# Search for the 256th score: thresholds and base formed on ScalarE instead of VectorE

## The chip, the cores and the metric

The kernel runs on one core of a Trainium2 chip. The core has five engines, each with its own queue of instructions that it works off in order: TensorE (PE, matrix products, with its weight loads shown as PEld), VectorE (DVE), ScalarE (ACT), GpSimd (POOL) and SyncE (SP, which only starts transfers here). They wait for each other by semaphores. The metric is the time of one execution on the device, in microseconds (us); the time before is the median of three runs.

## The reference

Two layers of a small transformer on 2048 tokens of width 512, in float32. Layer 0 adds a linear attention and a mixture of 16 experts to its input. Layer 1 adds a causal softmax attention over a window of 1024 and a block that works only on the highest-scoring eighth of the tokens. The change lies in that last block, where the 256 tokens are chosen (its weights' names shortened):

```python
xn = _layernorm(x, axis=-1)
x = x + attn(xn, ...) + ffn(xn, ...)
# in ffn:
k = max(1, int(T * CAPACITY))                        # 256
scores = jnp.einsum('btd,d->bt', hidden_states, w_router)
_, idx = jax.lax.top_k(scores, k)
idx = jnp.sort(idx, axis=-1)
sel = hidden_states[b, idx]
...
output = hidden_states.at[b, idx].set(gated.reshape(B, k, D))
```

What must come out of the search is the set of the 256 highest of 2048 scores, ties to the earlier token.

## The kernel before

The kernel goes through stages: layer 0 (to about 720 us in the profiled execution), then a stage here called the projections (720 to about 1010 us), the work on the chosen tokens, and last the attention of layer 1.

The projections run over 16 tiles t of 128 tokens. For each tile PE forms three products of 128 x 512, q, k and v (`p`, line 965, four quarters each, two passes per quarter), into a ring of three PSUM buffers. `normed_qk` normalises q and k: ACT squares (`t`, 754), DVE sums (`rr`, 755), ACT takes the root (78), DVE inverts (79) and multiplies (`qk`, 758), POOL applies the rotary embedding (763 to 773). One tile later `turned_qk` transposes them on PE (`trqk`, 110), and ACT copies the result out of PSUM (117) into qT and kT. The next tile's input is transposed in the same way (`tr`, copy to `xnt`).

Beside this two other pieces of work are threaded through the same tiles, step by step, at places written out in the loop:

- `early`, the row maxima of the attention to come (`maxima`): PE forms scores `pa` (633, masks 639 and 641) in one PSUM buffer, DVE reduces them to `mx` (645). Each pa waits for the mx before it. Per tile a few small reductions (`nm`, `parts`, 649 to 653) follow, then a transpose on PE (`tn`, 658).
- `route`, the choice of the tokens (`routing`). The scores are turned into whole numbers that order the same, split into a high half and a low half of 16 bits. `largest` finds the 256th largest of 2048 such numbers in three rounds, first for the high half (names ending in _h), then for the low half (_l). Each number of a round is tried by one partition: partition p forms the threshold base + step x (p + 1) (`thr`, 850; `steps` holds step x (p + 1)), compares all 2048 values with it and counts them (`ge`, `cnt`, 853), and notes whether there are at least 256 (854). A product with a matrix of ones on PE (`pc`, 859) sums the 128 notes into every partition; base rises by that sum times the step (860). The steps are 512, 4 and 1. The 2048 values come to every partition by way of DRAM: `row_d` is written from the scores' layout and read back as `row`, once for each half, by SP's transfers.

After the high half POOL forms the candidates of the low half from base (`low`, `above`, 867 to 870), and after the low half the set and the places (873 and on).

Four kinds of result share one PSUM buffer, `ps_t` with the tag "tr" and one buffer: tr, trqk, tn and pc. PE can write the next of them only when the one before has been read.

The code is written in one order, but the instructions of each engine are put in order by a scheduler when the kernel is built, so that a change of engine can also move instructions around it. At run time each queue is fixed.

Of the kernel before, what the change touches and what calls it, by code (L numbers as in the profile page):

```python
# [14 lines left out]
AF = mybir.ActivationFunctionType  # L15
ALU = mybir.AluOpType
# [22 lines left out]
def two_layer_kernel(ctx: ExitStack, tc: tile.TileContext, a: dict, out: bass.AP):  # L39
    nc = tc.nc  # L40
    V, S, G, PE = nc.vector, nc.scalar, nc.gpsimd, nc.tensor
# [4 lines left out]
    def const(shape, name, pool=cpool, dtype=F32):  # L46
        return pool.tile(shape, dtype, tag=name, name=name)
# [21 lines left out]
    def load(eng, dst, src):  # L69
        eng.dma_start(out=dst, in_=src)  # L70
# [57 lines left out]
    with ExitStack() as l0:  # L128
# [15 lines left out]
        with ExitStack() as p1:  # L144
# [8 lines left out]
            def load_x(t):  # L153
# [24 lines left out]
                base=0, channel_multiplier=0,  # L178
# [158 lines left out]
        with ExitStack() as p3:  # L337
# [119 lines left out]
            steps = head.steps()  # L457
# [7 lines left out]
            for b in range(NTB):  # L465
                atT, sh, xl = head.atT, head.sh, head.xl
                if b < NTB - 1:
                    head = Head(b + 1)
                    steps = chain(steps, head.steps())
# [253 lines left out]
    with p4:  # L723
# [59 lines left out]
        def routing():  # L783
# [5 lines left out]
                base=0, channel_multiplier=-1,  # L789
# [19 lines left out]
            def small(name, n=NT, dtype=F32):  # L809
                return const([P, n], name, r5, dtype)  # L810

            STEPS = (512, 4, 1)
            steps = const([P, 3], "steps", r5)
# [25 lines left out]
            def largest(m, first, name):  # L839

                load(nc.sync, row_d, m)
                row = r5.tile([P, NT * P], F32, tag="row", name=f"row_{name}")
                load(nc.sync, row, row_d.rearrange("p t -> (p t)").partition_broadcast(P))
                base = small(f"base_{name}", 1)
                G.memset(base, float(first))
                for _ in range(4):
                    yield
                for k, step in enumerate(STEPS):
                    thr = wk.tile([P, 1], F32, tag="thr", name=f"thr_{name}{k}")
                    V.tensor_tensor(thr, steps[:, k : k + 1], base, ALU.add)  # L850
                    ge = r5.tile([P, NT * P], BF16, tag="ge", name=f"ge_{name}{k}")
                    cnt = wk.tile([P, 1], F32, tag="cnt", name=f"cnt_{name}{k}")
                    V.tensor_scalar(ge, row, thr, None, ALU.is_ge, ALU.add, accum_out=cnt)
                    V.tensor_scalar(cnt, cnt, K2 - 0.5, None, ALU.is_ge)
                    yield
                    yield

                    pc = ps_t.tile([P, 1], F32, tag="tr", name=f"pc_{name}{k}")
                    PE.matmul(pc, ones, cnt, start=True, stop=True)
                    V.scalar_tensor_tensor(base, pc, float(step), base, ALU.mult, ALU.add)  # L860
                    yield
                return base

            th = yield from largest(hi, -32768, "h")

            low, above = small("low"), small("above")
            G.tensor_scalar(low, hi, th, None, ALU.is_equal)
            G.tensor_tensor(low, low, lo, ALU.mult)
            G.tensor_scalar(above, hi, th, 1e6, ALU.is_gt, ALU.mult)
            G.tensor_tensor(low, above, low, ALU.add)  # L870
            tl = yield from largest(low, 1, "l")
            same, inc, turn = small("same"), small("inc"), small("turn")
            G.tensor_scalar(above, low, tl, None, ALU.is_gt)
# [634 lines left out]
```

## Time and profile before

| | |
|---|---|
| three runs | 1710.59, 1710.7, 1712.12 us |
| median | 1710.7 us |
| the profiled execution | 1707.93 us |
| its span, first to last instruction | 1706.2 us |
| mean granted clock of PE in it | 0.994 |
| 740 to 850 us: busy PE / DVE / ACT / POOL | 101.0 / 71.0 / 23.8 / 51.9 us of 110 |
| 850 to 960 us: the same | 105.5 / 72.0 / 23.9 / 64.7 us of 110 |

The durations of the search's own instructions in that execution:

| line | engine | what | count | us each |
|---|---|---|---|---|
| 850 | DVE | thr | 6 | 0.15 in three of high half; 0.15, 0.36 and 2.34 in low |
| 853 | DVE | compare and count, 2048 values | 6 | 2.33 to 2.35 |
| 854 | DVE | cnt | 6 | 0.15 |
| 859 | PE | pc, two passes | 6 | 0.28 to 0.34 |
| 860 | DVE | base | 6 | 0.15 |

The profile lists, for each group of instructions, what ended the idle time before it ("<-"). The time of an engine that is idle while it is not needed costs nothing; what counts here is the idle time of PE, and the share of its clock that was granted.

### The profile page before, as it was taken

The numbers are of one execution on the slowest core, as the hardware profiler recorded it, in microseconds if no ns is written. First come the engines' busy times: TensorE is split into PE (matmuls) and PEld (weight loads), VectorE is DVE, ScalarE is ACT, GpSimd is POOL, SyncE is SP. The second block draws the span as 40 slices with busy tenths as digits, with TensorE's granted clock in tenths as the row PEclk, the third lists the DMA queues.
The fourth block names the chain that finished last, engine by engine and source line by source line (L and its number), as shares of the span: only waits on it lengthen the run. The fifth ranks groups of instructions, "written<-read, shape, count | busy, mean of one in ns | idle before, by whom it ended". The sixth has DMA issues, their size and how long they took to land.

```text
span 1706.2 us, 20420 instructions
## 1 busy us (share of the span) xinstructions
PE 1658.3 (97%) x8114; PEld 744.2 (44%) x8114; DVE 972.9 (57%) x1240; ACT 596.2 (35%) x955; POOL 499.6 (29%) x398
## 2 busy tenths in 40 slices
PE   8999999999999999999999989999999999999999
PEld 3445444444444444444443434454564333433343
DVE  4755646344445544356566676775554477556565
ACT  3213333243253344222121220440100576447473
POOL 3230000000000200053565425230000677558584
PEclk9999999999999999999999999999899999999999
DMA  9411001120030431121011034112222300110101
GB/s 362 168 38 47 25 25 37 46 90 25 25 111 25 94 105 50 51 68 56 25 27 31 28 105 167 62 50 75 74 99 75 100 1 2 50 51 2 50 2 38
DMA packets 62384, 109.22 MB, mean 64 GB/s; under 512 B 12529, under 2 KB 14065, under 8 KB 61521
## 3 DMA queue, kind: packets, MB, share of 16 engines
q1 hardware_dynamic: 55856, 106.12, 18.4%
q0 software_dynamic: 1152, 1.21, 0.4%
q10 hardware_dynamic: 5280, 0.59, 0.4%
q8 instruction: 63, 1.03, 0.2%
q14 instruction: 33, 0.26, 0.1%
HBM read 86.24 MB, written 21.67 MB: 63 GB/s over the span
## 4 chain that ended last, share of the span: by engine, by line
PE 83%; DVE 10%; ACT 2%; issue 2%; POOL 1%; DMA 1%; SPq 0%; DVEq 0%; POOLq 0%; ACTq 0%
PE eg L492 6%; PE ea L494 6%; PE acc L478 6%; PE pa L633 6%; PE ps L1300 6%; PE p L965 6%; PE av L1374 6%; PE po L553 3%; PE pq L367 3%; PE po L1344 3%; PE gx L242 3%; DVE mx L645 3%; PE pk L288 2%; PE mg L1214 2%; PE pm L1229 2%; PE sg L403 2%
## 5 line engine op out<-in xcount | busy, mean ns | idle before, releaser
L645 DVE TENSOR_REDUCE mx<-pa 128x4 f32<-128x1536 f32 (+3 forms) x144 | 252.8, 1756 | 160.5 <-PE pa L641 77.6
L1407 POOL TENSOR_TENSOR acc<-acc,pt 128x1024 f32<-128x1024 f32 (+2 forms) x110 | 252.7, 2325 | 96.7 <-DVE acc L1407 43.4
L1334 ACT ACTIVATE pt<-ps 128x1024 f32<-128x1024 f32 (+3 forms) x208 | 181.4, 924 | 108.1 <-PE ps L1323 61.5
L1407 DVE TENSOR_TENSOR acc<-acc,pt 128x1024 f32<-128x1024 f32 (+1 forms) x80 | 144.4, 1833 | 103.8 <-POOL acc L1407 103.8
L633 PE MATMUL pa<-kT,qT 32*128 32x384 f32 (+3 forms) x1152 | 139.8, 539 | 17.9 <-DVE mx L645 17.4
L350 ACT ACTIVATE r_e<-eg 128x512 f32<-128x512 f32 x128 | 75.8, 594 | 202.2 <-PE eg L492 195.7
L1300 PE MATMUL ps<-qT,kT 32*128 32x512 f32 (+3 forms) x1152 | 139.9, 525 | 0.0
L352 DVE TENSOR_TENSOR h<-ea,r_e 128x512 f32<-128x512 f32 x128 | 87.1, 684 | 85.1 <-ACT r_e L351 84.1
L743 POOL TENSOR_TENSOR cosg<-cosg,gam 128x512 f32<-128x512 f32 x2 | 2.5, 1264 | 442.6 <-DVE gam L740 442.6
L492 PE MATMUL eg<-xl,rwgT 128*128 128x512 f32 x256 | 130.8, 592 | 0.0
L494 PE MATMUL ea<-xw,rw1T 128*128 128x512 f32 x256 | 130.7, 592 | 0.0
L478 PE MATMUL acc<-h,rw2T 128*128 128x512 f32 x256 | 129.3, 592 | 0.0
L965 PE MATMUL p<-w_qk,xnt 128*128 128x512 f32 x256 | 124.2, 608 | 2.0 <-DVE qk L758 1.9
L1374 PE MATMUL av<-pt,v 128*32 128x512 f32 (+3 forms) x1024 | 100.8, 482 | 0.0
L1300 PEld LDWEIGHTS ps<-qT,kT 32*128 32x128 f32 x1152 | 54.7, 183 | 94.6 <-issue 65.7
L633 PEld LDWEIGHTS pa<-kT,qT 32*128 32x128 f32 x1152 | 46.6, 184 | 101.8 <-DVE mx L645 69.2
L488 DVE TENSOR_TENSOR xw<-xw,xl 128x512 f32<-128x512 f32 x64 | 43.8, 685 | 82.4 <-DMA xw<-w_d 82.2
L351 ACT ACTIVATE r_e<-r_e 128x512 f32<-128x512 f32 x128 | 80.3, 629 | 5.5 <-ACT r_e L350 1.8
L478 PEld LDWEIGHTS acc<-h,rw2T 128*128 128x128 f32 x256 | 48.7, 190 | 61.2 <-issue 53.7
L494 PEld LDWEIGHTS ea<-xw,rw1T 128*128 128x128 f32 x256 | 48.7, 190 | 61.2 <-issue 59.3
L492 PEld LDWEIGHTS eg<-xl,rwgT 128*128 128x128 f32 x256 | 48.7, 190 | 61.2 <-issue 60.7
L288 PE MATMUL pk<-k_wT,xnT 128*128 128x512 f32 x128 | 62.1, 629 | 3.6 <-ACT xnT L117 3.6
(336 smaller groups left out, 2419.7 us busy)
## 6 DMA issues: line engine op xcount, KB each, us to landing
xw<-w_d SPq DMA_DIRECT2D x64, 256.0 KB, 3.2
x<-in_x SPq DMA_DIRECT2D x16, 256.0 KB, 4.0
res_d<-x SPq DMA_DIRECT2D x16, 256.0 KB, 2.7
xr<-res_d SPq DMA_DIRECT2D x16, 256.0 KB, 4.1
xn_d<-xn SPq DMA_DIRECT2D x16, 256.0 KB, 2.9
res_d<-xr SPq DMA_DIRECT2D x16, 256.0 KB, 3.1
xnq<-xn_d SPq DMA_DIRECT2D x16, 256.0 KB, 2.7
v_d<-vt SPq DMA_DIRECT2D x16, 256.0 KB, 2.0
```

Source lines behind the costliest of these rows:

```text
L288: PE.matmul(pk, xt[:, c, :], k_wT[:, c, :], start=c == 0, stop=c == NC - 1)
L352: V.tensor_tensor(dst, pa, r, ALU.mult)
L478: PE.matmul(acc, rw2T[:, j, e, :], h, start=e == 0 and j == 0, stop=e == E - 1 and j == 1,)
L492: PE.matmul(pg, rwgT[:, e, hb], xl, start=True, stop=True)
L494: PE.matmul(pa, rw1T[:, e, hb], xw, start=True, stop=True)
L633: PE.matmul(pS[:, h, : w * P], qT[r, g, i * P : (i + 1) * P], kT[r, g, ks], start=True, stop=not (edge or last),)
L645: V.tensor_reduce(mx[:, g, :, c], pS[:, :, : w * P], AX.X, ALU.max)
L965: PE.matmul(pj, xnt[:, c, :], w, start=c == 0, stop=c == NC - 1)
L1300: PE.matmul(pS[h // 2][:, h % 2, t0 * P - q0 : (t1 + 1) * P - q0], kT[r, g, kb * P : (kb + 1) * P], qT[r, g, t0 * P : (t1 + 1) * P], start ...
L1334: S.activation(pT[:, :, :n], pS[hp][:, :, :n], AF.Exp)
L1374: PE.matmul(self.av[h * HD : (h + 1) * HD, t0 * P - o : (t1 + 1) * P - o], vs[kb // 4][:, kb % 4, hs], got[h // 2][:, h % 2, t0 * P - q0 : ...
L1407: eng.tensor_tensor(part, part, got[hp][:, :, : q1 - q0], ALU.add)
```

## The change

Two lines of `largest` change engine. The threshold was a DVE addition of `steps` and `base`; it becomes an ACT instruction, the identity function with base as its bias. The new base was a DVE instruction, pc x step + base; it becomes an ACT identity with step as scale and base as bias. Both act on one number per partition. The compare, the count and the product with ones stay.

```diff
@@ -847,7 +847,8 @@
                     yield
                 for k, step in enumerate(STEPS):
                     thr = wk.tile([P, 1], F32, tag="thr", name=f"thr_{name}{k}")
-                    V.tensor_tensor(thr, steps[:, k : k + 1], base, ALU.add)
+
+                    S.activation(thr, steps[:, k : k + 1], AF.Identity, bias=base)
                     ge = r5.tile([P, NT * P], BF16, tag="ge", name=f"ge_{name}{k}")
                     cnt = wk.tile([P, 1], F32, tag="cnt", name=f"cnt_{name}{k}")
                     V.tensor_scalar(ge, row, thr, None, ALU.is_ge, ALU.add, accum_out=cnt)
@@ -857,7 +858,7 @@
 
                     pc = ps_t.tile([P, 1], F32, tag="tr", name=f"pc_{name}{k}")
                     PE.matmul(pc, ones, cnt, start=True, stop=True)
-                    V.scalar_tensor_tensor(base, pc, float(step), base, ALU.mult, ALU.add)
+                    S.activation(base, pc, AF.Identity, bias=base, scale=float(step))
                     yield
                 return base
```

In the built program twelve instructions go from DVE's queue to ACT's, and the scheduler moves some others. On DVE the compare goes ahead of the small reductions (second round of the high half) and of the second qk (first round of the low half), and one mx goes ahead of rr of t=5. On PE trqk of the first and the third low round goes ahead of most of p<-w_v, one quarter of p<-w_qk behind two pa, and the products around pa of the next tiles shift by a quarter. On ACT the copy of qT goes ahead of the root of t=5. On POOL the rotary embedding of t=5 goes behind the first part of the routing after the low half. The lines after 850 have numbers greater by one in the changed kernel. Before and after these places the queues are the same.

## The prediction

> **What bounds the kernel now.** I read the page first, then TensorE's waits in the stretch of the search (740 to 850 us), then the timeline there, then the granted clock in slots of 3.4 us.
>
> ```profile
> span 1706.2 us, 20420 instructions
> PE 1658.3 (97%) x8114; PEld 744.2 (44%) x8114; DVE 972.9 (57%) x1240; ACT 596.2 (35%) x955; POOL 499.6 (29%) x398
> ```
>
> TensorE (PE) is busy for 97% of the span, so an edit is worth only what it takes from the idle time or the slow time of PE. The waits of PE, 740 to 850 us (line, who it waited for: us, times, longest):
>
> ```profile
> PE pa L633 <- DVE mx L645: 3.7, 3, 2.2
> PE trqk L110 <- DVE base_l L860: 3.3, 2, 2.1
> PE p L965 <- DVE qk L758: 1.9, 2, 1.6
> ```
>
> All of them end on VectorE (DVE), which also runs the search. The first can be due to the compare L853 ahead of the reduction mx; the second is the search itself. The timeline (start, us, engine, line, what; idle time in brackets):
>
> ```profile
> 761.28 2.35 POOL L763 TENSOR_TENSOR t<-qk,cosg 128x1024 f32<-128x1024 f32 x1 [8.16 <-DVE base_h L860]
> 761.31 2.34 DVE L850 TENSOR_TENSOR thr_l<-steps,base_l 128x1 f32<-128x1 f32 x1
> 763.57 2.33 DVE L853 TENSOR_SCALAR_CACHE_REDUCE ge_h<-row_h,thr_h 128x2048 bf16<-128x2048 f32 x1
> 766.02 1.22 DVE L645 TENSOR_REDUCE mx<-pa 128x4 f32<-128x1024 f32 x1
> 767.29 0.71 PE L633 MATMUL pa<-kT,qT 32*128 32x256 f32 x8 [0.87 <-DVE mx L645]
> ...
> 784.65 1.24 PE L633 MATMUL pa<-kT,qT 32*128 32x384 f32 x8 [2.20 <-DVE mx L645]
> ...
> 798.57 0.15 DVE L860 SCALAR_TENSOR_TENSOR base_l<-pc_l,base_l 128x1 f32<-128x1 f32 x1
> 798.87 0.63 PE L110 MATMUL trqk<-ident,qk 128*128 128x128 f32 x4 [1.26 <-DVE base_l L860]
> ...
> 817.65 0.15 DVE L860 SCALAR_TENSOR_TENSOR base_l<-pc_l,base_l 128x1 f32<-128x1 f32 x1
> 817.95 0.63 PE L110 MATMUL trqk<-ident,qk 128*128 128x128 f32 x4 [2.06 <-DVE base_l L860]
> ```
>
> First, an add of one number per partition (thr_l) took 2.34 us: it began 0.03 us after a GpSimd (POOL) tensor_tensor and ended with it; its siblings took 0.15 us. Second, the transposes trqk wait until base_l has read pc, since pc, tr, trqk and tn share one PSUM buffer (ps_t4, bufs=1), and base_l stands in DVE's queue behind a reduction of 1.75 or 2.28 us. The clock (stretch, us, busy PE, PEld, DVE, ACT, POOL, granted clock, DMA share, GB/s):
>
> ```profile
> 781.70:785.10 3.40, 1.20 (x10) 0.31 (x8) 2.86 (x4) 0.00 (x0) 3.32 (x3) 1.00 0.00 0
> 785.10:788.50 3.40, 3.40 (x17) 1.54 (x10) 1.76 (x1) 0.14 (x1) 0.51 (x1) 0.51 0.00 0
> ...
> 815.90:819.30 3.40, 1.35 (x12) 0.73 (x12) 1.90 (x2) 0.58 (x1) 3.40 (x3) 1.00 0.00 0
> 819.30:822.70 3.40, 3.40 (x14) 1.74 (x11) 2.23 (x1) 0.37 (x1) 3.32 (x2) 0.50 0.00 0
> ...
> 962.70:966.10 3.40, 1.61 (x8) 0.40 (x6) 2.91 (x5) 0.79 (x2) 0.00 (x0) 1.00 0.00 0
> ```
>
> After a slot in which PE was busy for 1.20 or 1.35 us, the next runs at half clock; after 1.61 us it did not here. So the two long gaps each cost a slow slot too. Its price by the timeline at 818.5: pa to the next p takes 1.71 us (1.31 at 807.42), two half-products 1.82 (0.86), four transposes 0.76 (0.50): 1.6 us.
>
> **The change, part by part.** Six thr (L850, DVE 0.15 us) and six base (L860, DVE 0.15 us) go from DVE to ScalarE (ACT); DVE keeps the six compares (2.34 us each) and six cnt. On ACT neither operation is in the trace. The nearest rows are the square root with a pointer as bias, 128x1, 294 ns, and the copy of 128x16 out of PSUM (ties), 172 ns; I take 0.30 for each, as the bias is a pointer here too, and 0.18 from PE's end to ACT's start (tr ends at 750.98, its copy starts at 751.16). The low end would bring each base 0.13 us sooner, the high end, rr's 321 ns, 0.02 later: under 0.4 us over three waits. ACT is busy for 23.8 of 110 us there, and the instruction order of the changed program adds no table load. A wait of ACT for pc holds up what follows it on ACT; I followed the order through, 0.03 to 0.1 us per handover, times of the trace of before:
>
> - Second round, 755 us: base and thr on ACT end at 755.2, so the compare starts as before (755.3). But nm (L649), 650 and 651 now come after it, ahead of rr: rr starts 0.3 late, qk and so PE's p at 760.59 too: **+0.3**.
> - Third round, 761 us: thr_l no longer waits for POOL. qk ends at 761.4, the compare starts at 761.5 instead of 763.57, mx at 764.4 (pa is ready then) instead of 766.02, and PE finds it done: **-0.87**.
> - base_h at 772.26 waited for mx (771.12); on ACT it ends 1.2 us sooner, so low and the two row transfers also start 1.2 sooner, and the compare for which DVE waited (row_l, 1.35 us) starts at 779.2 instead of 780.39. PE arrives 0.6 sooner as well, so its gap of 2.20 falls only to 1.6: **-0.6**. If the transfer lands no sooner it is 0; if all of 1.2 counts, -1.2.
> - First low round: trqk is now placed after one quarter of p<-w_v instead of three, and base_l on ACT behind rr (L78), which ends at 795.81: base ends at 796.1, the quarter at 795.65. Gap 1.26 becomes 0.6: **-0.66**. The compare goes ahead of the second qk here (2.4 us later); its buffer is wanted only some 5 us later, and POOL's rope of 7.2 us (763 to 773) still ends 4 us ahead of its transposes. Hidden; without that cover 2.4.
> - Second low round: a quarter of p<-w_qk moves behind pa_2, so PE comes to pa_2 0.86 sooner than before and waits for mx behind the compare: 0.65 instead of 0.1, **+0.55**.
> - Third low round: base_l directly follows the square of t=5 on ACT, trqk waits 0.2 instead of 2.06: **-1.86**. But ACT's copy of qT now precedes rr (L78), and mx of pa_2 precedes rr on DVE, so the last mx is later, and pa_0 of the next tile waits 0.3: **+0.3**. POOL's rope for t=5 moves behind the ten-odd small routing steps; it then ends at about the old time against a use 10 us later: 0.
>
> Sum of the idle time: 0.3 - 0.87 - 0.6 - 0.66 + 0.55 - 1.86 + 0.3 = -2.84. Both slow slots should go: 0.2 us of idle cannot halve the clock, and a gap of 1.6 leaves 1.8 busy in its slot, over the 1.61 that passed: -3.2. In all **-6.0 us**: 1706.2 to 1700.2 in the span of this execution (it ran 1707.93 in all). The three timed runs have their median at 1710.7, 2.8 above that execution; the difference is taken off it: **1704.7**. Bounds: a slot costs from 0 (not drawn) to 1.7 (half of 3.4), and the later gaps of about 1.8 us (964 us: full clock kept; 1000.6 us: lost) move against the slots by the gain, so one slot may come or go there: 1.6 either way.
>
> **The rivals.** (a) *The clock does not follow the gaps.* The rows for it: 1.61 us of busy time kept the full clock at 962.7 but lost it in 1000.2 to 1003.6. Then the slow slots stay and only idle time goes: 1710.7 - 2.84 = 1707.9. This is also what a rule of the Trainium skill would make of it, "TensorE: Matmul & The Clock Gate", section "Why this matters for your kernels": drops come from idle gaps above some 3 us. By that rule no gap here, 2.20 at most, should cost a slot; the trace shows two that did.
>
> (b) *The compare remains the pace.* It stays on DVE, 2.34 us, and now stands ahead of nm and qk. If the gaps at 784.65 and 798.87 stay whole, with the first slow slot, and the three new stops double from 1.15 to 2.3: -0.87 - 1.86 - 1.6 + 2.3 = -2.0: 1708.7. For it: PE's 3.7 us on mx; against it: DVE is busy for 71 of 110 us.
>
> (c) *Slower: ACT's queue holds the one PSUM buffer.* ACT works in order, and base now stands behind rr or a square that waits for others; while it waits, no tr, trqk or tn can be written. If base comes as late as rr does in the third low round (815.4 instead of 813.44: 1.9 us) in all three low rounds, with the slow slots kept: 3 x 1.9 - 0.87 - 0.6 = +4.2: 1714.9. It decides once base starts more than 2.06 us after pc, the longest such gap now. For it: the small operation is dearer on ACT (294 against 150 ns); against it: ACT is idle for 78% here and the order puts base first in two of three rounds. The Trainium skill speaks against the move too: "ScalarE: Activation LUTs", section "Rules for kernel authors", gives adds and multiplies to VectorE. By the rows that alone would be 12 x 0.144 = 1.7 us, were all on the path.
>
> (d) *It does nothing it says*: the numbers are the same whole numbers, so only if all of it were covered: 1710.7.
>
> **How the numbers follow.** The forecast 0.52, (a) 0.12, (b) 0.19, (c) 0.15, (d) 0.02. The forecast's own range is 1701 to 1707.3, from the slots and the transfer. Within 0.2% is 1707.3 to 1714.1, about what a measurement of this kernel can tell from no change. Faster: 0.52, half of (a), a little of (b): 0.60. Slower: (c), 0.15. Same: 0.25. The range of 8 in 10 reaches from 1700.5 (all row time counts, 1.2, a later slot goes too) to 1713.0, leaving out (c) and a little below.
>
> **What would show it.** Right: no thr of 2.3 us on any engine; base on ACT within 1 us of pc; the gap at 817.95 under 0.5 and full clock after it; the compare at 780 about 1 us sooner. Wrong: the waits of PE on mx between 740 and 850 us above 5 us, trqk waiting for ACT for over 1 us, or slots at half clock in the same number as before. The whole forecast falls if PE's idle time to 850 us does not shrink.

## The result and the profile after

On the chip of the first runs the changed kernel takes 1704.58 us (median of 8 runs, 1703.0 to 1710.8) against 1710.77 us (8 runs, 1708.05 to 1712.2): ratio 0.9974, 95% interval 0.9962 to 0.9986, which is 2.4 to 6.5 us less. Repeated on another chip the medians are 1703.80 and 1707.81 us, ratio 0.9973 (0.9964 to 0.9983). The profiled execution ran 1704.56 us; its page begins so (span, then busy time, share and instructions of each engine):

```profile
span 1702.2 us, 20423 instructions
PE 1655.0 (97%) x8114; PEld 742.2 (44%) x8114; DVE 969.9 (57%) x1228; ACT 598.4 (35%) x967; POOL 499.3 (29%) x398
```

The twelve instructions are on ACT. The waits of PE from 740 to 850 us (line, who it waited for: us, times, longest):

```profile
PE p L966 <- DVE qk L758: 2.3, 2, 1.8
PE pa L633 <- DVE mx L645: 2.1, 2, 1.8
PE tn L658 <- DVE parts L653: 0.4, 1, 0.4
PE trqk L110 <- ACT base_l L861: 0.2, 1, 0.2
```

They sum to 5.0 us, where the three shown of before made 8.9. The row of trqk behind base fell from 3.3 to 0.2, that of pa behind mx from 3.7 to 2.1; p behind qk did not fall. The timeline of the changed kernel at the same places (start, us, engine, line, what; idle time before in brackets):

```profile
762.75 0.27 ACT L861 ACTIVATE base_h<-pc_h,base_h 128x1 f32<-128x1 f32 x1
763.05 0.29 ACT L851 ACTIVATE thr_h<-steps,base_h 128x1 f32<-128x1 f32 x1
763.25 0.28 ACT L851 ACTIVATE thr_l<-steps,base_l 128x1 f32<-128x1 f32 x1
763.38 2.35 DVE L854 TENSOR_SCALAR_CACHE_REDUCE ge_h<-row_h,thr_h 128x2048 bf16<-128x2048 f32 x1
763.52 2.36 POOL L763 TENSOR_TENSOR t<-qk,cosg 128x1024 f32<-128x1024 f32 x1 [9.87 <-DVE qk L758]
...
781.28 2.35 DVE L854 TENSOR_SCALAR_CACHE_REDUCE ge_l<-row_l,thr_l 128x2048 bf16<-128x2048 f32 x1 [0.94 <-DMA row_l<-row_d]
785.54 0.93 PE L633 MATMUL pa<-kT,qT 32*128 32x384 f32 x8 [1.78 <-DVE mx L645]
795.36 0.63 PE L110 MATMUL trqk<-ident,qk 128*128 128x128 f32 x4 [0.21 <-ACT base_l L861]
809.16 1.14 PE L633 MATMUL pa<-kT,qT 32*128 32x512 f32 x8 [0.32 <-DVE mx L645]
812.07 0.26 ACT L861 ACTIVATE base_l<-pc_l,base_l 128x1 f32<-128x1 f32 x1
812.47 0.63 PE L110 MATMUL trqk<-ident,qk 128*128 128x128 f32 x4
```

The reader is to see four things. No thr takes 2.3 us, and the compare of the third round (763.38) stands directly behind its threshold. The gaps of 1.26 and 2.06 us ahead of the transposes are 0.21 us and nothing (the last line has no bracket). The gap of 2.20 us ahead of pa is still 1.78, because the compare there waits for its data: DVE is idle 0.94 us for row_l, 1.35 before. And ACT takes 0.26 to 0.29 us for each small operation.

The search stretch gains, and the next one gives some back (stretch, us, then busy PE, PEld, DVE, ACT, POOL, granted clock, DMA share, GB/s). The kernel before:

```profile
740.00:850.00 110.00, 101.00 (x506) 47.54 (x505) 70.95 (x92) 23.80 (x47) 51.85 (x64) 0.97 0.12 41
850.00:960.00 110.00, 105.48 (x508) 44.79 (x507) 72.03 (x68) 23.90 (x46) 64.67 (x54) 1.00 0.11 28
```

The changed kernel:

```profile
740.00:850.00 110.00, 104.95 (x542) 49.12 (x540) 71.48 (x89) 27.66 (x61) 54.58 (x66) 0.98 0.13 43
850.00:960.00 110.00, 103.81 (x496) 44.15 (x494) 71.04 (x63) 23.80 (x46) 62.81 (x52) 1.00 0.13 31
```

PE is busy 3.95 us more than before in the first stretch and 1.67 us less in the second. The waits of PE from 850 to 1020 us name the new one, which before did not have:

```profile
PE pa L633 <- DVE mx L645: 9.3, 9, 1.8
PE trqk L110 <- POOL qk L773: 2.6, 2, 2.2
```

It lies in the rotary embedding of tile 8, here in the changed kernel:

```profile
882.87 2.34 POOL L773 TENSOR_TENSOR qk<-t,t 128x1024 f32<-128x1024 f32 x1
885.26 0.66 PE L110 MATMUL trqk<-ident,qk 128*128 128x128 f32 x4 [2.17 <-POOL qk L773]
```

and here in the kernel before:

```profile
886.37 2.35 POOL L773 TENSOR_TENSOR qk<-t,t 128x1024 f32<-128x1024 f32 x1
888.77 0.66 PE L110 MATMUL trqk<-ident,qk 128*128 128x128 f32 x4
```

Before, POOL ended at 888.72 and PE began at 888.77 without a wait: just in time. After, PE was ready at 883.09, 5.7 us sooner; POOL ended at 885.21, only 3.5 sooner.

The clock in slots of 3.4 us, two stretches of the changed kernel:

```profile
743.40:746.80 3.40, 1.58 (x9) 0.58 (x7) 2.46 (x4) 1.28 (x3) 0.39 (x1) 1.00 0.21 77
746.80:750.20 3.40, 3.40 (x19) 1.67 (x22) 0.69 (x1) 0.00 (x0) 3.40 (x3) 0.50 0.02 5
...
883.30:886.70 3.40, 1.44 (x6) 0.69 (x6) 2.13 (x2) 1.17 (x3) 1.91 (x1) 1.00 0.00 0
886.70:890.10 3.40, 3.40 (x19) 1.65 (x19) 3.27 (x4) 0.06 (x1) 1.49 (x1) 1.00 0.00 0
```

The slots at half clock behind the two old gaps (785 and 819 us) are gone, and so is one behind a gap at 1002 us. A gap at 745 us, before the search's second round, costs one now, and the new gap at 885 us did not in this execution.

Half or more of what these two executions lose to the clock is lost elsewhere. Near 1200 us, long after the search, both kernels run for three slots on end at half clock (before, then after):

```profile
1190.00:1215.00 25.00, 22.15 (x97) 11.61 (x96) 12.08 (x14) 6.72 (x12) 0.00 (x0) 0.80 0.13 43
1190.00:1215.00 25.00, 22.15 (x102) 12.96 (x100) 12.37 (x15) 7.04 (x13) 0.00 (x0) 0.80 0.12 42
```

That is about 5 us each. In all thirteen profiles of this document the clock of this stretch is 0.73 to 0.86, a loss of 3.5 to 6.8 us. No experiment here touches it.

### The profile page after: what moved, and what is told of

It reads as the page before. It is cut to its first block, busy times and chain, and to the rows that moved or that the text cites. A ratio compares the mean times of both kernels' runs of the same rounds, so it can differ in the third digit from the quotient of the medians.

```text
span 1702.2 us, 20423 instructions
## 1 busy us (share of the span) xinstructions
PE 1655.0 (97%) x8114; PEld 742.2 (44%) x8114; DVE 969.9 (57%) x1228; ACT 598.4 (35%) x967; POOL 499.3 (29%) x398
## 4 chain that ended last, share of the span: by engine, by line
PE 80%; DVE 9%; POOL 3%; DMA 2%; ACT 2%; issue 2%; SPq 0%; DVEq 0%; POOLq 0%; ACTq 0%
PE eg L492 6%; PE ea L494 6%; PE acc L478 6%; PE ps L1301 6%; PE pa L633 6%; PE av L1375 6%; PE p L966 5%; PE po L553 3%; PE pq L367 3%; PE po L1345 3%; PE gx L242 3%; DVE mx L645 3%; PE mg L1215 2%; PE pm L1230 2%; PE po L555 2%
```

## The experiments

Two numbers are given for each kernel, since the slots at half clock are drawn anew in each execution and spread the times of one kernel over 3 to 10 us. The median and the ratio are the time itself. The *full-clock time* is the span of each run times its mean granted clock, averaged over the runs: what the span would be with no slow slot. It is an estimate, good to some 0.2 to 0.7 us by the scatter of its mean. "Lost" is the mean of span minus full-clock time. The kernels of one chip are held against the runs of the kernel before on that chip.

| kernel | runs | median us | ratio (95%) | lost us | full-clock us | against before |
|---|---|---|---|---|---|---|
| chip A: before | 27 | 1706.52 | | 7.3 | 1697.7 | |
| e1_thr_act | 11 | 1708.64 | 1.0014 (1.0005 to 1.0023) | 9.9 | 1696.9 | -0.8 |
| e2_base_act | 11 | 1704.77 | 1.0000 (0.9990 to 1.0010) | 8.8 | 1694.5 | -3.2 |
| e3_thr_one | 11 | 1704.77 | 0.9992 (0.9982 to 1.0003) | 7.4 | 1696.2 | -1.5 |
| e4_after_z5 | 5 | 1699.38 | 0.9964 (0.9950 to 0.9978) | 6.8 | 1692.0 | -5.7 |
| chip B: before | 27 | 1707.81 | | 8.0 | 1698.0 | |
| e5_after_again | 10 | 1703.80 | 0.9973 (0.9964 to 0.9983) | 7.7 | 1694.9 | -3.2 |
| e6_after_held | 12 | 1702.99 | 0.9974 (0.9963 to 0.9985) | 7.8 | 1693.5 | -4.6 |
| e7_hyb_z5_held | 5 | 1699.60 | 0.9948 (0.9935 to 0.9961) | 6.8 | 1690.9 | -7.1 |
| e8_before_z5 | 12 | 1709.49 | 1.0002 (0.9993 to 1.0011) | 8.8 | 1698.2 | +0.2 |
| chip C: before | 23 | 1707.28 | | 7.9 | 1697.3 | |
| e9_after_thrice | 12 | 1704.11 | 0.9987 (0.9975 to 0.9999) | 7.7 | 1694.7 | -2.6 |
| e10_hyb_z5 | 8 | 1701.80 | 0.9971 (0.9956 to 0.9985) | 7.2 | 1692.7 | -4.6 |
| e11_after_z5_again | 8 | 1700.79 | 0.9963 (0.9951 to 0.9975) | 6.4 | 1692.3 | -5.0 |

The profiled executions give a second measure of the queues. It is the time from the p that waits for qk at 745.21 us to two later pa, those at 875.00 and 910.98 us in the kernel before, less 1.7 us (half of 3.4) for each slot at half clock in between. The wait for POOL near 885 us lies between the two pa. It is an estimate from one execution each; two profiles of one kernel differ in it by up to 0.4 us.

| kernel | to the pa ahead of POOL's wait | to the pa behind it |
|---|---|---|
| before | 126.4 | 162.4 |
| e1_thr_act | 125.9 | 161.9 |
| e3_thr_one | 125.7 | 161.7 |
| e2_base_act | 122.8 | 159.0 |
| after | 121.7 | 159.8 |
| e5_after_again | 121.8 | 159.8 |
| e4_after_z5 | 121.6 | 157.6 |
| e11_after_z5_again | 121.2 | 157.2 |
| e10_hyb_z5 | 121.6 | 157.6 |
| e9_after_thrice | 123.2 | 159.2 |

### One half of the change alone: the threshold

```diff
-                    V.tensor_tensor(thr, steps[:, k : k + 1], base, ALU.add)
+                    S.activation(thr, steps[:, k : k + 1], AF.Identity, bias=base)
```

> Only the threshold on ScalarE, base stays on VectorE. The order on PE is that of the kernel before. Theory (two separate parts; the threshold was held by GpSimd's use of the shared path): thr_l is 0.3 us and no longer 2.34, the compare of the third high round starts 2 us sooner, PE's wait of 0.87 us on mx near 767 goes, the two waits of trqk on base_l (1.26 and 2.06 us) and the clock slots behind the long gaps stay. Time 0.9 us under before, 1709.8. Rival (it is the whole change that counts, or load on VectorE in general): half of the gain, 3 us, 1707.7.

The blocked threshold goes, and with it the wait at 767 us, but the three gaps stay (timeline of this kernel):

```profile
783.97 0.93 PE L633 MATMUL pa<-kT,qT 32*128 32x384 f32 x8 [2.54 <-DVE mx L645]
798.25 0.63 PE L110 MATMUL trqk<-ident,qk 128*128 128x128 f32 x4 [1.26 <-DVE base_l L860]
817.33 0.63 PE L110 MATMUL trqk<-ident,qk 128*128 128x128 f32 x4 [1.70 <-DVE base_l L860]
```

0.8 us of full-clock time is gained, the size of the wait removed (0.87), and 0.5 us in the traces. Part of it is spent at once: the gap ahead of pa at 784 grows from 2.20 to 2.54 us. The median rose, with 9.9 us lost to the clock, and the ratio's interval lies above 1; this half alone is no gain in time.

### The other half alone: the base

```diff
-                    V.scalar_tensor_tensor(base, pc, float(step), base, ALU.mult, ALU.add)
+                    S.activation(base, pc, AF.Identity, bias=base, scale=float(step))
```

> Only base on ScalarE, thresholds stay on VectorE. The order on PE is that of the changed kernel. Theory: trqk's waits on base_l fall to 0.2 us each, row_l comes about 1 us sooner, the slot at half clock behind the old gap of 2.06 goes, but thr_l or thr_h in the third high round still takes over 2 us because GpSimd began first, and the wait of about 0.9 us on mx there stays. 5 us under before, 1705.7, so most of the gain. Rival (VectorE's load in general): 3 us, 1707.7.

```profile
760.83 0.16 DVE L850 TENSOR_TENSOR thr_h<-steps,base_h 128x1 f32<-128x1 f32 x1
760.90 0.15 DVE L850 TENSOR_TENSOR thr_l<-steps,base_l 128x1 f32<-128x1 f32 x1
761.05 2.37 POOL L763 TENSOR_TENSOR t<-qk,cosg 128x1024 f32<-128x1024 f32 x1 [8.12 <-DVE thr_l L850]
...
792.34 0.63 PE L110 MATMUL trqk<-ident,qk 128*128 128x128 f32 x4 [0.21 <-ACT base_l L860]
807.80 1.14 PE L633 MATMUL pa<-kT,qT 32*128 32x512 f32 x8 [1.98 <-DVE mx L645]
```

The timeline of this kernel shows the gap ahead of trqk at 0.21 us, as in the whole change; in its place PE waits 1.98 us for mx at 807.80, where it waited 2.06 for base 10 us later before. The expectation that the threshold would stay blocked on DVE failed: the scheduler put thr_l first and POOL's operation starts as it ends, so it takes 0.15 us. Full-clock time falls by 3.2 us, as much as by the whole change. The time itself is not shown to fall (ratio 1.0000, the median 1.75 us lower, where 5 was expected): this kernel's runs lost 8.8 us to the clock and those before 7.3.

That the base alone does as well as the whole change is due in part to the wait for POOL near 885 us, which is 0.50 us in this kernel and 2.17 in the changed one. Ahead of that wait the traces give 3.6 us for the base alone, 4.7 for the whole change and 0.5 to 0.7 for the threshold alone. So the base's place in a queue is the main cause of the gain, some three quarters of it in the search, and the threshold adds a part of the rest, where it meets POOL.

### The threshold mended without ScalarE

```diff
-                    V.tensor_tensor(thr, steps[:, k : k + 1], base, ALU.add)
+                    V.tensor_scalar(thr, steps[:, k : k + 1], base, None, ALU.add)
```

> The kernel before, with the threshold still on VectorE but written with one tensor operand and base as the per-partition scalar instead of two tensors. Same engines, same order on PE. Theory (only an operation with two tensors in SBUF waits for GpSimd): no thr over 0.2 us, the wait of 0.87 us near 767 goes, 0.9 us under before, 1709.8, as in the run with only the threshold on ScalarE. Rival (VectorE is held for another reason, such as the semaphore of base_l): thr_l stays at 2.3 us, time as before, 1710.7.

The sum is the same, but the instruction reads one tensor, and base as a pointer to one number per partition. DVE and POOL in its timeline:

```profile
760.56 2.36 POOL L763 TENSOR_TENSOR t<-qk,cosg 128x1024 f32<-128x1024 f32 x1 [8.10 <-DVE base_h L860]
760.65 0.20 DVE L850 TENSOR_SCALAR thr_l<-steps,base_l 128x1 f32<-128x1 f32 x1
760.77 2.34 DVE L853 TENSOR_SCALAR_CACHE_REDUCE ge_h<-row_h,thr_h 128x2048 bf16<-128x2048 f32 x1
```

thr_l starts 0.09 us after the same POOL operation that held it for 2.34 us before, and takes 0.20. So it was the form with two tensors that waited for POOL, not DVE as such. This is what the Trainium skill says ("SBUF — State Buffer", section "Who interferes with whom"): a VectorE instruction with two inputs from SBUF waits for a GpSimd one that reads SBUF, one with a single input does not. The gain is 1.5 us of full-clock time against 0.8 with the threshold on ACT. The means' scatter of 0.2 to 0.4 leaves it open whether these two differ, and by the traces they do not (161.7 and 161.9). The time is not shown to fall (0.9982 to 1.0003).

### The wait for POOL near 885 us

The list of chosen tokens is written by 16 indirect transfers that POOL issues in four groups, at some 0.97 us each, threaded through the tiles. One more step between the groups lets the rotary embedding of tile 8 go ahead of a group:

```diff
-                for _ in range(4):
+                for _ in range(5):
```

> The changed kernel, with five steps instead of four between the groups of list transfers, which puts the last group of four behind the rotary embedding of t=8 on GpSimd; nothing else moves. Theory (the new wait of trqk on GpSimd, 2.17 us at 885, is GpSimd's queue: the embedding of t=8 stands behind eight transfers of 1.27 us): the wait goes, 2 us under the changed kernel, 1702.5. Rival (PE then waits for something else just behind, mx or the next embedding): 1704.6.

> A repeat of the changed kernel with one more step between the groups of list transfers, on the same chip as the run before it, to hold that one against. The wait of trqk for POOL near 885 us stays under 0.5 us, span times granted clock 1691.5 to 1693, 5 to 6 us under the kernel before; median 1698 to 1702, by how many slots at half clock the executions draw.

```profile
875.32 2.35 POOL L773 TENSOR_TENSOR qk<-t,t 128x1024 f32<-128x1024 f32 x1
883.24 0.63 PE L110 MATMUL trqk<-ident,qk 128*128 128x128 f32 x4
```

In the first of the two kernels' timelines POOL ends 5.6 us before PE comes, and PE does not wait. Full-clock time is 5.7 and in the repeat 5.0 us under the kernel before, where the whole change alone had 3.2 (each on another chip, with 0.2 to 0.7 us of scatter). By the traces the step gains 2.2 to 2.6 us up to the pa behind the wait, and 0.1 to 0.6 up to the one ahead of it. The same step in the kernel before tells whether that wait was there already:

> The kernel before with only the list transfers moved behind the embedding of t=8. Theory (in the kernel before, that embedding ends just in time, 888.72 against PE at 888.77, so it costs nothing there and becomes a wait only when PE comes sooner): under 0.5 us by span times clock, no change of the median beyond 1 us. Rival (the transfers always cost): 2 us less.

It was not: +0.2 us of full-clock time, nothing that can be told from zero (ratio 1.0002; the median is 1.7 us higher, where at most 1 was expected, with 8.8 us lost to the clock and 8.0 before). So the change itself turned cover that was just enough into a wait of 2.2 us, and about 2 us of its gain go there.

### The changed kernel again

> The changed kernel again, beside the kernel before on the same chip as the parts. The kernel before gave 1706.5 us there and 1710.8 on the first chip, so a part of the first difference may be slots at half clock that fell otherwise. Theory (the queue part of the gain is firm, 2 to 3 us; the slots are drawn anew in each execution): span times granted clock 2 to 3 us under that of before (1697.7), 1695.2, and a median 2 to 5 us under before. Rival (the whole 6 us are firm): a median 6 us under before, and span times clock 6 us under too.

The waits are those of the first profile. The clock drew other slots; stretches of this kernel as above:

```profile
882.99:886.40 3.41, 1.10 (x6) 0.69 (x6) 2.55 (x2) 0.79 (x2) 2.39 (x2) 1.00 0.00 0
886.40:889.80 3.40, 3.40 (x15) 1.31 (x14) 1.79 (x4) 0.61 (x2) 0.94 (x1) 0.51 0.00 0
```

The same gap for POOL, 2.31 us here, costs a slot in this execution and cost none in the first, where it fell less fully into one slot (1.10 us of busy time against 1.44). Over the runs the changed kernel loses 7.7 us to the clock and the kernel before 8.0: the loss is nearly the same.

### The gap at 745 us

Here p waits for qk of tile 1, since the search's first compare (740.55 to 742.9 in the changed kernel) stands ahead of it on DVE. To put it behind, the first base of the high half is made from zero times qk of tile 1, plus its constant:

```diff
+            if t == 1:
+                V.tensor_scalar(held[0][0], qk[:, 1, 0, 0:1], 0.0, held[0][1], ALU.mult, ALU.add)
...
-                G.memset(base, float(first))
+                if name == "h":
+                    held.append((base, float(first)))
+                else:
+                    G.memset(base, float(first))
```

> The changed kernel with the first base of the high half formed from a normalised q or k of tile 1 times zero, so that the first compare, which waits for the transfer of row_h, stands behind rr and qk of that tile on VectorE and not ahead of them. Theory (the idle time of PE at 745, 0.9 to 2.2 us from run to run, is VectorE held by that transfer, and draws a slow slot when long): the wait of p on qk there goes, span times clock falls by 1 to 2 us against the changed kernel, the median by 2 to 3. Rival (PE only comes sooner to the next wait, at 763 or 785, which are set by the transfer of row_l and by GpSimd): under 0.5 us.

```profile
747.91 0.50 PE L633 MATMUL pa<-kT,qT 32*128 32x128 f32 x8 [1.38 <-DVE cnt_h L860]
```

The gap at 745 us is gone, and PE waits 1.38 us for the search 2 us later. Full-clock time falls by 1.4 us against the changed kernel on the same chip, and the wait for POOL, 0.85 us here instead of 2.31, could alone be all of it. The median falls by 0.8 us, where 2 to 3 was expected, and the ratio to the kernel before is the same (0.9974 and 0.9973): no gain in time is shown for the held compare.

### Where ScalarE is needed, and a version that beats both

With the base on ACT, the threshold back on DVE in its one-tensor form, the added step, and then the held compare too:

```diff
-                    S.activation(thr, steps[:, k : k + 1], AF.Identity, bias=base)
+                    V.tensor_scalar(thr, steps[:, k : k + 1], base, None, ALU.add)
...
-                for _ in range(4):
+                for _ in range(5):
```

> The changed kernel with one more step between the groups of list transfers, and thr back on VectorE as an addition with base as a pointer to one number per partition (one tensor read). Only base is on ScalarE. If ScalarE's thr is what gains, this loses about 0.8 us of full-clock time against the kernel with thr on ScalarE and the same step; if only base's place counts, it is the same within 0.7 us: span times granted clock 1691 to 1693, median 1699 to 1701. No thr above 0.25 us, though POOL's rope may run beside it.

> The candidate to beat both: base on ScalarE, the threshold on VectorE in the form with one tensor, the last list transfers behind the embedding of t=8, and the first compare behind the normalisation of tile 1. Theory: the parts add, span times clock 2.5 for base and threshold, 2 for the list transfers and 1.5 for the first compare under the kernel before, 1691.7, the median 7 to 9 under before. Rival (each part only uncovers the next wait): no better than the changed kernel with the list transfers moved, 1692.0 and 7 under.

Without the held compare it has the full-clock time of the kernel with both operations on ACT and the same step (1692.7 and 1692.3 on one chip, 0.3 and 0.2 us of scatter each): ScalarE for the threshold is worth some 0.4 us by either measure, no more than their scatter. With the held compare 1690.9 us, and a ratio of 0.9948 (0.9935 to 0.9961): the lowest of all, 8 us under the kernel before and clear of the changed kernel on the same chip. That it is faster than the changed kernel with the added step is not shown, since the intervals overlap.

### A handover made dearer

```diff
+                    for again in range(3):
+                        spare = wk.tile([P, 1], F32, tag="spare", name=f"spare_{name}{k}{again}")
+                        S.activation(spare, pc, AF.Identity, bias=base, scale=float(step))
                     S.activation(base, pc, AF.Identity, bias=base, scale=float(step))
```

> The changed kernel with three spare activations of one number per partition on ScalarE ahead of each base, on the same operands (the result is not used): each base comes about 0.8 us later after pc (3 x 0.27 by the row of base), so the handover through ScalarE is four times as dear. Theory (ScalarE has slack of the size of the gap that the transposes had, and only waits set the time): base is on the way to a transpose trqk in two low rounds, where the wait was 0.2 and 0: 2 x 0.6 to 0.8 more, and in the three rounds in which the next compare follows at once, up to 0.8 each if TensorE then waits for mx, so full-clock time rises by 1 to 3 us over the changed kernel, median 1704 to 1708. Rival (c) of the prediction (ScalarE's queue holds the one PSUM buffer, everything behind it waits too): the rise is over 4 us, with trqk waiting for base for over 1 us three times. The scheduler also moves a quarter of a product here and there, so under 1 us either way says nothing.

```profile
810.15 0.55 ACT L863 ACTIVATE spare_l<-pc_l,base_l 128x1 f32<-128x1 f32 x3
810.72 0.26 ACT L864 ACTIVATE base_l<-pc_l,base_l 128x1 f32<-128x1 f32 x1
811.23 0.60 PE L110 MATMUL trqk<-ident,qk 128*128 128x128 f32 x4
...
814.27 1.14 PE L633 MATMUL pa<-kT,qT 32*128 32x512 f32 x8 [1.58 <-DVE mx L645]
```

The timeline shows three in a row taking 0.55 us together, not 0.8, since one starts before the other has ended. No trqk waits for base; the scheduler had also placed this one behind two quarters of p, where the changed kernel has one. PE's waits from 740 to 850 us rise from 5.0 to 6.7 us, all of the rise at mx (3.8 instead of 2.1). The order near 885 us moved as well, and the wait for POOL fell to 0.34 there. The full-clock time, 1694.7, is that of the changed kernel (1694.9 and 1695.5), so the two cancel and the price of the handover can't be read from it. In the traces, ahead of the wait for POOL, this kernel takes 1.4 to 1.5 us more than the changed one, and its longer waits are those for mx; what of this is the later base and what the other order was not separated. What can be read: in this order a base 0.6 us later does not hold the transposes.

## Why the prediction came out right, step by step

The time was met, 1704.58 against 1704.7, but not every term of its sum was, and that it was met to 0.1 us is luck.

**The profiled pair.** The sum was made for the profiled execution, 1706.2 to 1700.2 us of span; it came to 1702.2. By the first lines of the two pages PE's idle time, span minus busy, fell from 47.9 to 47.2 us, by 0.7 where 2.84 was forecast. Its busy time fell by 3.3, about the price of two slots at half clock (six before, four after), as forecast. The medians differ by 6.2 us, and 2.8 of this is only that the execution profiled before ran faster than its median, while the one profiled after ran at its median. So this pair alone would give nearly all of the gain to the clock. The runs on chip B, 27 and 10, give it to the queues instead: 3.2 us of full-clock time and 0.3 of the clock. The traces stand between, with 2.6 us of queues behind the wait for POOL.

**The idle time of the search: right in its causes, larger in size.** Forecast and measured, in the two profiled executions: second high round +0.3, measured +0.1 (p waits 0.48 us); third, without POOL's block, -0.87 and -0.9; row_l -0.6 and -0.42 (2.20 to 1.78); first low round -0.66 and -1.05; second low +0.55 and +0.2 (pa waits 0.32); third low -1.86 and -2.06; pa_0 of the next tile +0.3 and nothing. In sum -4.1 instead of -2.84. Base starts sooner after pc than the 0.18 us taken where ACT is free: 0.05 us at 756.58. The latest base was 0.8 us behind its pc (794.19 to 794.98), as it stood behind rr; it starts 0.09 us before that rr has ended, where 0.03 to 0.1 after it was taken. That the base carries most of it is shown by e2, and that the threshold's block was a matter of its form with two tensors by e3.

**Row_l.** The step said the compare would come 1.2 us sooner and PE 0.6: the compare is bounded by its transfer, and DVE's idle time before it fell by 0.41 us only. The view that said so was the 1.35 us of idle time before that compare, and the step had named this as its bound.

**"POOL's rope" called hidden: the step that failed.** It was followed for tiles 4 and 5 and not for tile 8, where the list transfers stand ahead of it. There the cover in the profile of before was 0.05 us, and PE now comes 5.7 us sooner: +2.2 us, shown by e4 and e11 (wait gone, and 5.0 and 5.7 us under the kernel before in place of 3.2) against e8 (nothing). With it the idle time sums to -4.1 + 2.2 = -1.9 in the profiled pair. What is left to the -0.7 of the pages lies outside the search: 0.4 us more in layer 0, and 0.9 more ahead of a tn at 1002 us, where the kernel before was in a slow slot. Over the runs the full-clock time fell by 3.2 us on chip B. So the -2.84 was close to that because a gain that was too small and a loss left out cancelled.

**The two slow slots, -3.2: mis-sized.** The slots at the two old gaps did go: none of the nine profiles with the base on ACT has one there. But the time lost to the clock is 7.7 us a run after and 8.0 before on chip B, a change of 0.3. The stretch near 1200 us loses 3.5 to 6.8 us in every profile; with its 5 us in the profile of before, about 3 of the 8.0 are left for all other gaps, and these draw slots in other executions (746.8 in the first profile, 886.4 in the repeat). Nor did the old gaps cost a slot each time: 2.48 us at 783 in e3 and 1.70 at 817 in e1 cost none. So a slot saved at one place was worth its price in this execution only. The kernels with the added step and the base on ACT lost 6.4 to 7.2 us, but e1 and e2 lost 9.9 and 8.8, with up to 0.9 us of scatter in each mean: what the term is over many runs is not shown, beyond that chip B gives 0.3 and not 3.2.

**The median taken as base.** 1710.7 was 2.8 us above the profiled execution, and the forecast took -6.0 off it. On three further chips the kernel before has medians of 1706.5 to 1707.8, near that execution. The difference of the medians is -6.2 on the first chip and -4.0 on chip B; the mean falls by 3.7 there, 3.2 of it full-clock time. Both agree with the interval of 2.4 to 6.5 us; what the first chip showed beyond the 3.7 is taken for the draw of slots, which its runs of before, of which only times are known, can't confirm.

**The rivals.** (a), that only idle time goes, has about the right size for chip B (-2.84 against -3.7 of the means), though not for its reason: the short slots do follow gaps. The rule of the Trainium skill that it cited ("TensorE: Matmul & The Clock Gate", section "Why this matters for your kernels": gaps above some 3 us drop the clock) does not hold here: 2.31 us did. What the same page says of the activity window, that it runs freely and does not start with the kernel (section "What's actually happening"), agrees with the same gap costing a slot in one execution and none in another. (b) was half true: the gap at 784 us stays at 1.78, because of the transfer, but PE's waits on mx fell to 2.1 us. (c), ACT's queue holding the PSUM buffer, would have begun at a base 2.06 us behind pc; the latest was 0.8. With three spare operations ahead of each base it still did not appear, but base came at most 1.4 us behind pc there, so a base later than 2.06 us was never tried.

**The marks named ahead.** Thr, base within 1 us of pc and the gap at 817.95 came as said. The compare at 780 came 0.4 us sooner against the work around it, not 1. The number of short slow slots fell in the profiled pair from three (785, 819 and 1003 us) to one, and in the repeat's profile it was again three (145, 886 and 910 us).

## What to carry to other kernels

Where several small results share one PSUM buffer, the reader that frees it belongs on the queue that reaches it soonest, even if the operation itself costs more there: 0.26 us on ACT in place of 0.15 on DVE, and two waits of 3.3 us in all became 0.2. When PE gets ahead in one stretch, look up every operation after it that ended within that gain of its use, on all queues: such a pair of lines without a wait between them is the next wait. A DVE operation on two tensors beside POOL is worth rewriting with a pointer to a scalar, before it is moved to another engine: here that took 0.20 us in place of 2.34, though the kernel's time is not shown to fall by it alone.

## What the runs showed of the hardware

- In the rows of 3.4 us shown here a slot at half clock follows one in which PE was busy for 1.10 to 1.58 us, and the bound is not the busy share alone: the slot with 1.58 us of busy PE at 743.4 lost the next slot's clock, the one with 1.44 us at 883.3 kept it (both above). What else counts was not tried.
- The spread of a kernel's times is mostly this draw: in the runs of before, a longer span goes with a lower granted clock, with a correlation of 0.89 on each of chips A, B and C.
- A single number per partition on ACT costs 0.24 to 0.30 us, but three in a row 0.55 us.
